# Eight weight matrices loaded as 32 runs of 16 KB and put in order by two block transpositions, in a kernel that streams 128 MB through one core

## The chip, the core and the metric

The kernel runs on one core of a Trainium2 chip. The metric is the device time of one execution in microseconds (us). Before the change it is 324.08 us, the median of 3 runs that lie between 323.89 and 324.3 us.

## What is computed

There are 128 images of 128 channels by 1024 columns in float32 (64 MiB in all), one subject number from 0 to 7 for each image, and eight weight matrices of 128x128 in float32, one for each subject. Each image is multiplied by the matrix of its subject, and the image itself is added:

```
w = weights[subjects]                        # B, C, D = 128, 128, 128
out = jnp.einsum('bct,bcd->bdt', x, w)       # T = 1024
x = x + out
```

The images are read once (67.1 MB) and the results are written once (67.1 MB). The eight matrices together are 0.5 MB.

## The kernel before, in words

The work goes in 32 turns of four images each (H = 2 halves of G = 2 images). A ring of 12 slots in SBUF (`x_all`, `xs`, 2 MB for each slot) holds the images: a turn's images are loaded into its slot, the result is written over them in place, and the slot is stored from there.

Two queues issue the DMAs. ScalarE (ACT) issues the loads, one for each image, through the helper `transfer` (L50), which passes the shapes of both sides to the DMA as they are written: on the side of DRAM an image is 32 rows of 16 KB, on the side of SBUF 128 partitions of 4 KB. The first 48 loads fill the 12 slots and wait for nothing; from turn 12 on ACT waits until a slot's store has landed (L200 to L203). SyncE (SP) issues, in this order: the 128 subject numbers (`given`, L179), the eight matrices (`w_all`, L180), and then the stores, each as soon as VectorE has added the half or the slot that it takes (L217). Most stores take a slot whole; the first and the last turn are stored in parts, and the last image by itself at the end (L238).

The matrices come with one `dma_start` into `w_all`: partition c holds row c of every matrix, which is 1024 pieces of 512 bytes. VectorE brings the subject numbers into range (L193 to L198), waits for the matrices (L222), reads the first four subject numbers into its registers (`subjects_of`) and copies the four matrices into the stationary tiles `ws` (`place`, L150 to L153). TensorE waits for the copy (`s_go`) and for the images (`s_ready`, which GpSimd passes on) and multiplies (`multiply`, L155); VectorE adds the product out of PSUM to the images in place (`add`, L170, L173), copies the matrices of the next turn (L152), and so on in a loop of 32 turns on each of the two engines (`nc.vector.Fori` at L226, `nc.tensor.Fori` at L231). Ahead of this TensorE multiplies zeros (L185) while nothing has landed yet.

The lines that the change and the steps of the prediction touch: the load of the matrices (L180), the wait for them (L222), the copies (L152), the operand of the multiplication (L161), and the issue of loads by ACT between L199 and L205.

Of the kernel before, what the change touches and what calls it, by code (L numbers as in the profile page):

```python
# [30 lines left out]
G = 2  # L31
H = 2
# [3 lines left out]
SLOTS = 12  # L36
# [3 lines left out]
DMA = 16  # L40
# [2 lines left out]

ROWS = 4

ALIGN = 4096
QUEUES = {mybir.EngineType.SP: "qSPDynamicHW", mybir.EngineType.Activation: "qActDynamicHW"}

# [21 lines left out]
@with_exitstack  # L70
def kernel(
    ctx: ExitStack,
    tc: tile.TileContext,
    x: bass.AP,
    subjects: bass.AP,
    weights: bass.AP,
    out: bass.AP,
):
    nc = tc.nc
    B, C, T = x.shape  # L80
    S, _, D = weights.shape
    NT = B // (G * H)

    def sbuf(name, *shape, dtype=F32):
        return ctx.enter_context(nc.sbuf_tensor(name, list(shape), dtype)).ap()


    room = -(nc.sbuf_base + -nc.sbuf_base % 32) % ALIGN
    if room:
        sbuf("room", C, room // 4)  # L90
    x_all = sbuf("x_all", C, SLOTS * H * G * T)
    xs = [
        x_all[:, i * H * G * T : (i + 1) * H * G * T].rearrange("c (q t) -> c q t", t=T)
        for i in range(SLOTS)
    ]
    w_all = sbuf("w_all", C, S, D)
    ws = [sbuf(f"w{i}", C, 1, D) for i in range(H * G)]
    zeros = sbuf("zeros", C, N)
    given, near, wrap = (sbuf(name, 1, B, dtype=I32) for name in ("given", "near", "wrap"))
    index = sbuf("index", 1, B + H * G, dtype=I32)  # L100
    ps = [
        ctx.enter_context(nc.psum_tensor(f"ps{i}", [D, G, T], F32)).ap() for i in range(P_SLOTS)
    ]

    s_given = tc.alloc_semaphore("s_given")
    s_wall = tc.alloc_semaphore("s_wall")
    s_index = tc.alloc_semaphore("s_index")
    s_zeros = tc.alloc_semaphore("s_zeros")
    s_product = tc.alloc_semaphore("s_product")
    s_added = tc.alloc_semaphore("s_added")  # L110

    s_ready = tc.alloc_semaphore("s_ready")
    s_go = tc.alloc_semaphore("s_go")

    s_slot = [tc.alloc_semaphore(f"s_slot{k}") for k in range(SLOTS)]
    s_head = tc.alloc_semaphore("s_head")
    s_first = tc.alloc_semaphore("s_first")

    def emptied(i):
        turns = i // SLOTS  # L120
        return DMA * (H * G + 1) * turns - (DMA * G if i >= SLOTS and i % SLOTS == 0 else 0)

    def load(engine, i, q):
        transfer(
            nc,
            engine,
            xs[i % SLOTS][:, q, :],
            x[i * H * G + q].rearrange("(a r) t -> a (r t)", r=ROWS),
        ).then_inc(s_head if i * H * G + q < G else s_slot[i % SLOTS], DMA)

    def store(i, q0, q1):
        b = i * H * G
        transfer(
            nc,
            nc.sync,
            out[b + q0 : b + q1].rearrange("g d t -> d g t"),
            xs[i % SLOTS][:, q0:q1, :].rearrange("d (o g) t -> d o (g t)", g=min(G, q1 - q0)),
        ).then_inc(s_first if i == 0 and q1 == G else s_slot[i % SLOTS], DMA)

    def subjects_of(i):  # L140
        _, subject = nc.values_load_multi_w_load_instructions(
            index[0:1, i] if isinstance(i, slice) else index[0:1, bass.ds(i * (H * G), H * G)],
            engines=[mybir.EngineType.DVE],
            min_val=0,
            max_val=S - 1,
            skip_runtime_bounds_check_because="the index is clamped on the chip above",
        )
        return subject

    def place(h, subject):  # L150
        for q in range(h * G, (h + 1) * G):
            copy = nc.vector.tensor_copy(ws[q], w_all[:, bass.ds(subject[q], 1), :])  # L152
        copy.then_inc(s_go, 1)  # L153

    def multiply(slot, h):  # L155
        nc.tensor.wait_ge(s_go, 1).then_inc(s_go, -1)
        nc.tensor.wait_ge(s_ready, 1).then_inc(s_ready, -1)  # L157
        for q in range(h * G, (h + 1) * G):
            for t in range(0, T, N):
                at = slot * (H * G * T) + (q * T + t)  # L160
                mm = nc.tensor.matmul(  # L161
                    ps[h][:, q % G, t : t + N],
                    ws[q][:, 0, :],
                    x_all[:, bass.ds(at, N)],
                    start=True,
                    stop=True,
                )
        mm.then_inc(s_product, 1)

    def add(slot, h):  # L170
        mine = x_all[:, bass.ds(slot * (H * G * T) + h * G * T, G * T)]
        nc.vector.wait_ge(s_product, 1).then_inc(s_product, -1)  # L172
        nc.vector.tensor_tensor(  # L173
            mine, ps[h].rearrange("d g t -> d (g t)"), mine, ALU.add
        ).then_inc(s_added, 1)

    with tc.tile_critical():  # L177

        nc.sync.dma_start(given, subjects.rearrange("(o b) -> o b", o=1)).then_inc(s_given, DMA)  # L179
        nc.sync.dma_start(w_all, weights.rearrange("s c d -> c s d")).then_inc(s_wall, DMA)  # L180

        nc.vector.memset(zeros, 0.0).then_inc(s_zeros, 1)  # L182
        nc.tensor.wait_ge(s_zeros, 1)
        for _ in range(IDLE):
            nc.tensor.matmul(  # L185
                ps[P_SLOTS - 1][:, G - 1, :N], zeros[:, :D], zeros, start=True, stop=True
            )

        nc.vector.memset(index[:, B:], 0).then_inc(s_index, 1)  # L192
        nc.vector.wait_ge(s_given, DMA)  # L193
        nc.vector.tensor_scalar(near, given, -S, S - 1, ALU.max, ALU.min).then_inc(s_index, 1)  # L194
        nc.vector.wait_ge(s_index, 2)
        nc.vector.tensor_scalar(wrap, near, 0, S, ALU.is_lt, ALU.mult).then_inc(s_index, 1)  # L196
        nc.vector.wait_ge(s_index, 3)
        nc.vector.tensor_tensor(index[:, :B], near, wrap, ALU.add).then_inc(s_index, 1)  # L198
        for i in range(NT):  # L199
            if i == SLOTS:  # L200
                nc.scalar.wait_ge(s_first, DMA)
            if i >= SLOTS:
                nc.scalar.wait_ge(s_slot[i % SLOTS], emptied(i))  # L203
            for q in range(H * G):
                load(nc.scalar, i, q)  # L205

        for i in range(NT):
            if i == 0:
                nc.gpsimd.wait_ge(s_head, DMA * G).then_inc(s_ready, 1)
                nc.gpsimd.wait_ge(s_slot[0], DMA * G).then_inc(s_ready, 1)  # L210
            else:
                nc.gpsimd.wait_ge(s_slot[i % SLOTS], emptied(i) + DMA * H * G).then_inc(s_ready, H)

        for i in range(NT):
            for h in range(H):
                if i in (0, NT - 1) or h == H - 1:
                    nc.sync.wait_ge(s_added, i * H + h + 1)  # L217
                    store(i, h * G if i in (0, NT - 1) else 0, (h + 1) * G - (i * H + h == NT * H - 1))


        nc.vector.wait_ge(s_index, 4)
        nc.vector.wait_ge(s_wall, DMA)  # L222
        subject = subjects_of(slice(0, H * G))
        for h in range(H):
            place(h, subject)
        with nc.vector.Fori(0, NT) as turn:  # L226
            subject = subjects_of(turn + 1)
            for h in range(H):
                add(turn % SLOTS, h)
                place(h, subject)  # L230
        with nc.tensor.Fori(0, NT) as turn:  # L231
            for h in range(H):
                multiply(turn % SLOTS, h)

    with tc.tile_critical() as waits:
        for i in range(NT - SLOTS, NT):
            nc.scalar.wait_ge(s_slot[i % SLOTS], emptied(i + SLOTS) + (DMA if i == NT - 1 else 0))
    last = nc.sync.dma_start(out[B - 1], xs[(NT - 1) % SLOTS][:, H * G - 1, :])  # L238

    tc.add_manual_dep(  # L240
        last.ins,
        waits.name,
        mybir.DependencyInfo(mybir.DependencyClass.NoSync, mybir.DependencyReason.SCHED_ONLY),
        reason="the end of the program waits for it",
    )
# [27 lines left out]
```

## Time and profile before

| | |
|---|---|
| median of 3 runs | 324.08 us |
| the profiled execution, its own time | 324.3 us |
| its span, from first to last instruction | 322.5 us |
| mean granted clock of TensorE | 0.92 |
| busy: TensorE, VectorE | 237.1 us (74%), 165.7 us (51%) |
| time that packets of the two DMA queues took, share of 16 engines' span | 50.0% (q1) and 49.5% (q10) |
| matrices: DMA issued, landed after | 1.35 us, 5.2 us |
| first and last copy of a matrix (L152) | 7.41 us, 281.1 us |
| first multiplication of an image (L161) | 8.56 us |
| first and last issue of a store | 16.40 us, 301.89 us |

The page of the profile is one execution on the chip. Its first part gives the busy time of each engine, the second cuts the span into 40 equal slices and writes the busy share of each in tenths (9 is 90% or more), with the share of the 16 DMA engines and the GB/s that they moved in two rows of their own. The third gives the DMA queues: packets, megabytes, and the time that their packets took as a share of the span of 16 engines. The DMA view can be asked for a stretch of time; it then cuts that stretch into 40 slices and counts the packets that started in it. The times in texts are microseconds from the start of the span.

The queue q1 is that of SP (subject numbers, matrices, stores), q10 that of ACT (images): q1 moved 67.64 MB, which is the 67.11 MB of the results and 0.53 MB of matrices and subject numbers; q10 moved the 67.12 MB of the images. A DMA is made of packets of data and, behind them, of packets of four bytes by which the engines that carried it report to its semaphore; the profile counts both.

### The profile page before, as it was taken

To read this page: it belongs to the slowest core of one execution; us is meant where nothing else is said; L and a number is where in the kernel's file an instruction comes from. 1 tells how busy PE (TensorE), PEld (TensorE's weight loads), DVE (VectorE), ACT (ScalarE), POOL (GpSimd) and SP (SyncE) were. 2 spreads that over 40 slices of the span, in tenths; PEclk is the share of its full clock that TensorE was granted. 3 is DMA by queue.
4 is the path that set the end of the run, shared out by engine and by line. 5 is a ranking of instruction groups with operands and counts; after the bars stand their busy time and mean duration, and the time that the engine had idled before them with its cause. 6 is when DMAs were issued, how large, how long until landed. Compare 5 with 4: busy or idle time off the path is not lost. (4 is left out here: it accounts for less than half of the span.)

```text
span 322.5 us, 2381 instructions
## 1 busy us (share of the span) xinstructions
PE 237.1 (74%) x518; PEld 98.1 (30%) x518; DVE 165.7 (51%) x202; POOL 0.2 (0%) x4
## 2 busy tenths in 40 slices
PE   5999998888888888888888888888885995500000
PEld 2434433333333333333333333333331432100000
DVE  2267776666566566666656655666666263600000
POOL 0000000000000000000000000000000000000000
PEclk9799999999999999999999999999999798955555
DMA  7999999999999999999999999999999999999996
GB/s 276 427 391 421 427 428 421 427 429 435 417 427 433 421 425 423 431 427 427 423 424 431 433 419 424 430 426 426 433 426 418 428 425 423 428 429 425 426 425 288
DMA packets 16067, 134.76 MB, mean 418 GB/s; under 512 B 2625, under 2 KB 3650, under 8 KB 3906
## 3 DMA queue, kind: packets, MB, share of 16 engines
q1 hardware_dynamic: 9922, 67.64, 50.0%
q10 hardware_dynamic: 6144, 67.12, 49.5%
q14 instruction: 1, 0.01, 0.0%
HBM read 67.63 MB, written 67.11 MB: 418 GB/s over the span
## 5 line engine op out<-in xcount | busy, mean ns | idle before, releaser
L161 PE MATMUL ps<-x_all,w 128*128 x512 | 232.7, 609 | 39.7 <-PEq L157 39.7
L173 DVE TENSOR_TENSOR x_all<-ps,x_all 128x2048 f32 x64 | 146.6, 2291 | 109.4 <-DVEq L172 109.4
L161 PEld LDWEIGHTS ps<-x_all,w 128*128 128x128 f32 x512 | 96.4, 193 | 176.0 <-issue 175.8
L152 DVE COPY w<-w_all 128x128 f32 x132 | 23.1, 218 | 4.2 <-DMA w_all<-in_L_cond_weights_dram 4.2
L185 PE MATMUL ps<-zeros 128*128 128x512 f32 x6 | 4.4, 890 | 1.7 <-DVE zeros L182 1.7
L185 PEld LDWEIGHTS ps<-zeros 128*128 128x128 f32 x6 | 1.7, 305 | 3.5 <-issue 1.9
L182 DVE MEMSET zeros<- 128x512 f32 x1 | 0.5, 485 | 1.0 <-SPq L177 1.0
L194 DVE TENSOR_SCALAR near<-given 1x128 int32<-1x128 int32 x1 | 0.2, 216 | 0.8 <-DMA given<-in_itok_B_dram 0.8
L198 DVE CUSTOM_DVE_ANT_0 index<-near,wrap 1x256 uint16<-1x256 uint16 x1 | 0.3, 278 | 0.0
L196 DVE TENSOR_SCALAR wrap<-near 1x128 int32<-1x128 int32 x1 | 0.2, 215 | 0.0
L260 POOL MEMSET const-bfloat16-1.0<- 128x1 bf16 x1 | 0.1, 101 | 0.0
L260 POOL MEMSET const-uint8-127<- 128x1 uint8 x1 | 0.1, 101 | 0.0
L260 POOL MEMSET const-float32-0.0<- 128x1 f32 x1 | 0.1, 98 | 0.2 <-issue 0.2
L260 POOL MEMSET const-float32-1.0<- 128x1 f32 x1 | 0.1, 98 | 0.0
L260 DVE BASE_LOAD x1 | 0.0, 15 | 0.1
L192 DVE MEMSET index<- 1x4 int32 x1 | 0.1, 62 | 0.0
## 6 DMA issues: line engine op xcount, KB each, us to landing
x_all<-in_x_dram ACTq DMA_DIRECT2D x128, 512.0 KB, 31.6
out_dram<-x_all SPq DMA_DIRECT2D x30, 2048.0 KB, 47.1
out_dram<-x_all SPq DMA_DIRECT2D x3, 1024.0 KB, 14.4
out_dram<-x_all SPq DMA_DIRECT2D x2, 512.0 KB, 20.6
w_all<-in_L_cond_weights_dram SPq DMA_DIRECT2D x1, 512.0 KB, 5.2
given<-in_itok_B_dram SPq DMA_DIRECT2D x1, 0.5 KB
```

The source lines that it names most:

```text
L152: copy = nc.vector.tensor_copy(ws[q], w_all[:, bass.ds(subject[q], 1), :])
L161: mm = nc.tensor.matmul(ps[h][:, q % G, t : t + N], ws[q][:, 0, :], x_all[:, bass.ds(at, N)], start=True, stop=True,)
L173: nc.vector.tensor_tensor(mine, ps[h].rearrange("d g t -> d (g t)"), mine, ALU.add).then_inc(s_added, 1)
L182: nc.vector.memset(zeros, 0.0).then_inc(s_zeros, 1)
L185: nc.tensor.matmul(ps[P_SLOTS - 1][:, G - 1, :N], zeros[:, :D], zeros, start=True, stop=True)
L192: nc.vector.memset(index[:, B:], 0).then_inc(s_index, 1)
L194: nc.vector.tensor_scalar(near, given, -S, S - 1, ALU.max, ALU.min).then_inc(s_index, 1)
L196: nc.vector.tensor_scalar(wrap, near, 0, S, ALU.is_lt, ALU.mult).then_inc(s_index, 1)
L198: nc.vector.tensor_tensor(index[:, :B], near, wrap, ALU.add).then_inc(s_index, 1)
L260: nc = _bacc.Bacc("TRN2", target_bir_lowering=False, num_devices=1)
```

## The change

The matrices are no longer loaded with row c of each in partition c. They are read in 32 runs of 16 KB (32 rows of a matrix, which lie side by side in DRAM, are one run; there are four such runs in each of eight matrices) through `transfer`, as the images are. On the side of DRAM the access is 4 by 8 runs of 16 KB, the four blocks of rows outermost and the eight matrices inside; on the side of SBUF it is 128 partitions of 4 KB, so that a run fills four partitions. Partition 32b + 4s + q then holds rows 32b + 8q to 32b + 8q + 7 of matrix s.

VectorE puts them in order. It transposes the 32x32 blocks of `w_runs` into `w_turned`, which lies in the last slot of the ring, waits for that, transposes the blocks back with their columns read in another order, and waits again. Row c of matrix s is then in partition c, in four pieces of 32 columns that lie 256 columns apart (`w_all`, the same memory as `w_runs`). `place` copies a matrix out of these four pieces. ACT waits for both transpositions before the loads of the last slot (turn 11), and the stationary tile is a plain 128x128.

```
+BLOCK = 32
...
-    w_all = sbuf("w_all", C, S, D)
-    ws = [sbuf(f"w{i}", C, 1, D) for i in range(H * G)]
+    w_runs = sbuf("w_runs", C, S * D)
+    w_all = w_runs.rearrange("c (h s l) -> c h s l", s=S, l=BLOCK)
+    w_turned = x_all[:, (SLOTS - 1) * H * G * T :][:, : S * D]
+    ws = [sbuf(f"w{i}", C, D) for i in range(H * G)]
...
-            copy = nc.vector.tensor_copy(ws[q], w_all[:, bass.ds(subject[q], 1), :])
+            copy = nc.vector.tensor_copy(
+                ws[q].rearrange("c (h o l) -> c h o l", o=1, l=BLOCK),
+                w_all[:, :, bass.ds(subject[q], 1), :],
+            )
...
-                    ws[q][:, 0, :],
+                    ws[q],
...
-        nc.sync.dma_start(w_all, weights.rearrange("s c d -> c s d")).then_inc(s_wall, DMA)
+        transfer(
+            nc,
+            nc.sync,
+            w_runs.rearrange("c (o f) -> c o f", o=1),
+            weights.rearrange("s (b r) d -> b s (r d)", r=BLOCK),
+        ).then_inc(s_wall, DMA)
...
+            if i == SLOTS - 1:
+                nc.scalar.wait_ge(s_wall, DMA + 2)
             if i == SLOTS:
                 nc.scalar.wait_ge(s_first, DMA)
...
         nc.vector.wait_ge(s_wall, DMA)
+        nc.vector.transpose(w_turned, w_runs).then_inc(s_wall, 1)
+        nc.vector.wait_ge(s_wall, DMA + 1)
+        nc.vector.transpose(
+            w_runs,
+            w_turned.rearrange("c (j a) -> c a j", j=RUN),
+        ).then_inc(s_wall, 1)
+        nc.vector.wait_ge(s_wall, DMA + 2)
         subject = subjects_of(slice(0, H * G))
```

## The prediction

> **What bounds the kernel now.** I first read the second and third parts of the page, because the kernel moves 134.76 MB and computes little.
>
> ```profile
> PE   5999998888888888888888888888885995500000
> ...
> DMA  7999999999999999999999999999999999999996
> ...
> DMA packets 16067, 134.76 MB, mean 418 GB/s; under 512 B 2625, under 2 KB 3650, under 8 KB 3906
> ...
> q1 hardware_dynamic: 9922, 67.64, 50.0%
> q10 hardware_dynamic: 6144, 67.12, 49.5%
> ```
>
> The 16 DMA engines are full in every slice but the first and the last, and the two queues' packets take 50.0 + 49.5 = 99.5% of 16 engines' whole span. TensorE has nothing left to do in the last five slices. So the end is not set by a chain of instructions (the chain of waits reaches back only to 278.56 us and shows nothing but small steps): it is set by how long the busiest DMA engine needs for the packets given to it. The table of stages says the same: from 281 to 322.5 us VectorE is busy for 0.30 us and TensorE not at all, while DMA runs at 399 GB/s. The stores are some 40 us behind the computation, and that is cover for anything that is late at the start.
>
> Next I asked the DMA view for three stretches: the matrices alone, a stretch of loads alone, and the end.
>
> ```profile
> DMA packets 1083, 0.97 MB, mean 358 GB/s; under 512 B 32, under 2 KB 1056, under 8 KB 1056
> ...
> q1 hardware_dynamic: 1040, 0.52, 65.1%
> ```
>
> This is 3.6 to 6.3 us. All 1040 packets of the matrices (1024 of 512 bytes, 16 that report) are in it and took 65.1% of 16 x 2.7 us = 28.1 us, or **1.76 us on each of 16 engines**.
>
> ```profile
> DMA packets 383, 4.19 MB, mean 419 GB/s; under 512 B 127, under 2 KB 127, under 8 KB 127
> ...
> q10 hardware_dynamic: 383, 4.19, 98.7%
> ```
>
> This is 6.3 to 16.3 us, loads of images alone: 383 - 127 = 256 packets of 16 KB in 98.7% of 160 us, 157.9 us, so **0.617 us for one 16 KB packet** (reports counted in).
>
> ```profile
> DMA  7399796998997999989989989977433212011000
> ...
> q1 hardware_dynamic: 321, 1.20, 73.0%
> ```
>
> This is 317 to 321 us in slices of 0.1 us. At 319.7 us the share falls to four tenths, and at 320.8 us it reaches nothing: most engines finish by about 319.8 us, and a few go on for about 1 us. The engines end that close to each other, after 320 us of work each, because every large DMA gives each engine the same share.
>
> **The load of the matrices.** It loses 1024 packets of 512 bytes and gains 32 of 16 KB. Whether this gains or loses depends on how many engines carry the 32 runs, which no row shows directly; the packet counts bound it. There are 2625 packets under 512 bytes. The issues listed on the page are 128 loads, 35 stores and the matrices, 164 DMAs, and 164 x 16 = 2624. The one packet that is left is the report of `given`. So 164 DMAs ran on 16 engines, and one ran on a single engine. What sets them apart is the outermost count of their accesses: the loads have 32 on one side and 128 on the other, the stores and the old matrices 128, `given` has 1. The new load has 128 in SBUF but **4 in DRAM** (the blocks of rows outermost). Its ends are then 4 engines with 8 runs each, if the outermost count is what is dealt out, and 16 engines with 2 runs each, if all 32 runs are, as in an image's load.
>
> - 4 engines: 8 x 0.617 = 4.94 us on each, where 1.76 us was: +3.18 us on four engines, -1.76 us on the twelve others.
> - 16 engines: 2 x 0.617 = 1.23 us on each: -0.53 us on all.
>
> I take 4: in every row the number of engines goes with the outermost counts, and a count of 4 on one side is nearer to the 1 of `given` than to the 32 of an image's load.
>
> The Trainium skill (DMA: Bandwidth & Descriptors, "Why a DMA increments its semaphore by 16 and not by 1") says that each side's slowest dimension that isn't 1 is looked at, and that the largest number up to 16 that divides both is the number of engines. By that rule the new load gets 4, and the trace agrees with it for 128 with 32 (16 engines) and for `given` (one). The same page ("Specifications") gives 512 bytes as enough for full rate; by it the old pieces would have cost 1.23 us like large ones, and the sum would be +3.71 us with 4 engines and nothing with 16. The trace does not agree, as 1.76 us is 43% more than 1.23 us, and the trace decides.
>
> **What the other engines can take over.** Nothing: which engine carries which part of an image is settled by the image's shape, so the four that are behind stay behind through all 128 loads and 35 stores, and both queues have work waiting throughout (a load lands 31.6 us after its issue, a store 47.1 us, by the medians on the page). The end moves by +3.18 us if the engine that ends last is one of the four, and by 3.18 less the 1.1 us of spread, about +2.1 us, if they are among the early ones. I take the middle, **+2.6 us**.
>
> **The two transpositions.** No row shows one. Each handles 1024 elements in a partition. By the fill of zeros (512 elements in 485 ns) it would take 0.97 us, by the addition (2048 in 2291 ns) 1.15 us, by the copy of a matrix (128 in 218 ns) 1.74 us: two of them 1.9 to 3.5 us. I take 2.3 us, by the addition, which is the row of nearest length. They lie between the landing of the matrices and the first copy. If the matrices go through back to back, as they do now, they land 8.7 to 9 us from the start instead of 6.55 (1.35 + 5.2); if they take turns with packets of images, by about 14 us. The first copy now comes 0.86 us after the landing, and the first multiplication 1.15 us after that copy. The first multiplication moves from 8.56 us to 13.3 us (9.0 + 2.3 + 0.86 + 1.15), or to 18 us at worst, and the first store from 16.40 us to 21 or 26 us. **Cost: nothing.** It is hidden by the loads, of which 48 are free to go: 25.2 MB, 60 us at 419 GB/s. By 26 us less than half of that has landed. Without this cover it would cost those 5 to 10 us. Late first stores let the loads run further ahead, and the same bytes follow at the end.
>
> **The waits.** VectorE's two new waits hold up only its own copies, which the last paragraph prices. ACT's wait before turn 11 stands ahead of loads 45 to 128. ACT issues 14 loads in 9.10 us, 0.65 us each, and reaches this wait at 0.9 + 44 x 0.65 = 29.5 us; the transpositions are over by 12 to 17 us. Cost nothing; if they came after 29.5 us there would still be a queue of loads issued and not carried out. SP's stores stand behind no new wait.
>
> **The copies.** 132 copies of 218 ns read four pieces of 32 columns instead of one of 128. No row shows such a copy. Below, nothing changes; above, I allow a doubling, 4 x 0.22 = 0.9 us more in a turn. A turn is about 10 us (320 over 32), of which VectorE works 165.7 / 32 = 5.2 us. Hidden by DMA, cost nothing; if DMA weren't the bound it would cost up to 28 us in all, as TensorE waits for the copies. The plain stationary tile changes no count.
>
> **The sum.** 324.3 us of the profiled execution + 2.6 = 326.9 us; the median lies 0.2 us lower, so **326.7 us**.
>
> **The rivals.**
>
> 1. All 16 engines carry the runs, two each, as they carry an image's 32. For it: the same helper, the same size of run, and 32 runs can be dealt out to 16. Against it: the outermost count, and `given`. It gives 324.08 - 0.53 = 323.5 us, not slower. The point at which the change turns from gain to loss is 1.76 / 0.617 = 2.9 runs on the busiest engine: up to two runs gain, three or more lose. With eight engines (four runs, 2.47 us) it would be +0.7 us, 324.8 us.
> 2. The limit is one that the engines share, not one of each: then four engines left alone at the end would go faster, and the 4.9 us by which they trail the twelve (3.18 + 1.76) would shrink. For it: loads alone (419 GB/s) and loads with stores (427 GB/s, 60 to 268 us) run at nearly one rate. Against it: 512 KB in small packets ran well below that rate (1.76 us an engine is 298 GB/s) and nothing filled the gap. With the last 4.9 us at double speed the end would come 2.4 us earlier, at 324.3 us.
> 3. The runs of the four engines run into other engines' writes to the same partitions, as each run fills four partitions that an image's share also fills. No row shows two engines on one partition. A run would take up to twice 0.617 us: +4.94 us more, 331.6 us.
> 4. The late start gets through to the end: product and first store 5 to 10 us late. It decides only where it exceeds the 40 us by which the stores trail; it would give up to 334 us. Everything in the stages after 281 us speaks against it.
>
> **How the numbers follow.** Four engines, end moved by 2.0 to 3.6 us: 0.72, the forecast, with a range of its own of 326.0 to 327.7 us. Sixteen engines: 0.13. Eight engines or a shared limit, 324.1 to 325.5 us: 0.07. Collisions or a start that gets through, 328 to 334 us: 0.08. The range is 323.4 to 328.5 us: it needs the other side as well to hold 8 in 10 safely, since the bounds of the number of engines are its ends. A measurement of this kernel can tell about 0.2%, 0.65 us, from no change. Faster by more than that needs 323.43 us or less, which only the lower edge of rival 1 reaches: 0.04. Within it: the rest of rival 1 and half of the eight engines: 0.13. Slower: 0.83.
>
> **What would show it.** With four engines q1 has 9922 - 1040 + 32 + 4 = 8918 packets and 2613 are under 512 bytes; with sixteen, 8930 and 2625. With four the stretch before the end has about 5 us in which the DMA share is near a quarter, and the matrices land about 7.5 us or more after their issue. Two transpositions of 1 to 1.7 us stand ahead of a first multiplication at 13 to 18 us, and TensorE and VectorE still have nothing to do in the last 35 us. The forecast is wrong if the matrices run on 16 engines, or if four lagging engines catch up before the end.

## The result, and the profile after

The changed kernel takes 332.84 us (median of 5 runs, 332.29 to 333.1) against 323.89 us before (5 runs, 323.77 to 324.3): 1.0274 times as long, 95% interval 1.0264 to 1.0285, or 8.95 us more. The forecast was 326.7 us, slower, with a range up to 328.5 us: the sign was right, and the size was a third of what came. The profiled execution took 332.87 us with a span of 331.1 us, 8.6 us more than the span before.

The page of the kernel before has this row, in slices of 8.06 us:

```profile
GB/s 276 427 391 421 427 428 421 427 429 435 417 427 433 421 425 423 431 427 427 423 424 431 433 419 424 430 426 426 433 426 418 428 425 423 428 429 425 426 425 288
```

The page of the changed kernel, first the rows of the slices and of the DMA queues, then the groups that are new:

```profile
DMA  6999999999999999999999999999999999999993
GB/s 180 238 374 424 420 434 421 426 427 425 428 428 425 428 427 424 426 428 427 426 428 424 424 437 417 427 437 423 424 422 437 416 421 428 427 427 427 427 423 161
DMA packets 15063, 134.76 MB, mean 407 GB/s; under 512 B 2613, under 2 KB 2614, under 8 KB 2870
...
q1 hardware_dynamic: 8918, 67.64, 48.8%
...
L161 DVE COPY w<-w_runs 128x128 f32 x132 | 23.2, 219 | 0.8 <-DVE w_runs L247 0.8
L245 DVE STREAM_TRANSPOSE x_all<-w_runs 128x1024 f32<-128x1024 f32 x1 | 1.2, 1245 | 16.6 <-DMA w_runs<-in_L_cond_weights_dram 16.6
...
L247 DVE STREAM_TRANSPOSE w_runs<-x_all 128x1024 f32<-128x1024 f32 x1 | 1.9, 1915 | 0.0
```

The number of engines is in the packet counts: 8918 on q1 and 2613 under 512 bytes are the numbers worked out for four engines; sixteen would have left 8930 and 2625. What no step of mine had is in the GB/s: DMA is full from the second slice on, as before, but the first three slices (8.3 us each) move 180, 238 and 374 GB/s, where it was 276, 427 and 391. In the second of them the engines are busy all the time and move little more than half as much. VectorE waits 16.6 us for the matrices (first transposition at 19.57 us), the first multiplication comes at 24.44 us and the first store at 33.78 us.

The DMA view from 4 to 18 us, before and after:

```profile
DMA packets 1469, 5.90 MB, mean 422 GB/s; under 512 B 173, under 2 KB 1139, under 8 KB 1139
...
q10 hardware_dynamic: 487, 5.41, 91.4%
```

```profile
DMA packets 266, 3.16 MB, mean 226 GB/s; under 512 B 73, under 2 KB 73, under 8 KB 73
## 3 DMA queue, kind: packets, MB, share of 16 engines
q10 hardware_dynamic: 235, 2.70, 83.4%
q1 hardware_dynamic: 31, 0.46, 13.7%
```

After the change the images' queue has 2.70 MB, 165 packets of 16 KB, in 83.4% of 16 x 14 us = 186.8 us: **1.13 us for a packet** that took 0.617 us before. The matrices' queue has 28 of its 32 runs in 13.7%, 30.7 us: 1.10 us for a run. In these 14 us 5.90 - 3.16 = 2.74 MB less were moved, which at 422 GB/s is 6.5 us of all 16 engines. From 18 us on the rate is 419 GB/s again.

The end of the changed kernel, 320 to 331.1 us in slices of 0.28 us:

```profile
DMA  9997999999999999853332212122222221000000
```

The share falls below a half at about 324.9 us, as twelve engines finish (at 319.8 us before, by the row in the prediction), and stays near two tenths, which is some four engines in sixteen, until about 329.3 us. So four engines do trail, by some 4.4 us, where 4.94 us was worked out. But the twelve end 5.1 us later than before, where they were to end 1.76 us earlier.

### The profile page after: what moved, and what is told of

It is laid out like the page before. It is cut to its first block, busy times and chain, and to the rows that moved or that the text cites. A ratio compares the mean times of both kernels' runs of the same rounds, so it can differ in the third digit from the quotient of the medians.

```text
span 331.1 us, 2383 instructions
## 1 busy us (share of the span) xinstructions
PE 241.9 (73%) x518; PEld 100.0 (30%) x518; DVE 168.9 (51%) x204; POOL 0.2 (0%) x4
## 2 busy tenths in 40 slices
DMA packets 15063, 134.76 MB, mean 407 GB/s; under 512 B 2613, under 2 KB 2614, under 8 KB 2870
## 3 DMA queue, kind: packets, MB, share of 16 engines
q1 hardware_dynamic: 8918, 67.64, 48.8%
## 5 line engine op out<-in xcount | busy, mean ns | idle before, releaser
L173 PE MATMUL ps<-x_all,w 128*128 x512 | 236.6, 619 | 43.7 <-PEq L169 26.2
L173 PEld LDWEIGHTS ps<-x_all,w 128*128 128x128 f32 x512 | 98.2, 197 | 182.7 <-issue 182.3
L161 DVE COPY w<-w_runs 128x128 f32 x132 | 23.2, 219 | 0.8 <-DVE w_runs L247 0.8
L245 DVE STREAM_TRANSPOSE x_all<-w_runs 128x1024 f32<-128x1024 f32 x1 | 1.2, 1245 | 16.6 <-DMA w_runs<-in_L_cond_weights_dram 16.6
L202 PE MATMUL ps<-zeros 128*128 128x512 f32 x6 | 5.3, 1057 | 1.7 <-DVE zeros L199 1.7
L247 DVE STREAM_TRANSPOSE w_runs<-x_all 128x1024 f32<-128x1024 f32 x1 | 1.9, 1915 | 0.0
```

The source lines that it names most:

```text
L161: copy = nc.vector.tensor_copy(ws[q].rearrange("c (h o l) -> c h o l", o=1, l=BLOCK), w_all[:, :, bass.ds(subject[q], 1), :],)
L173: mm = nc.tensor.matmul(ps[h][:, q % G, t : t + N], ws[q], x_all[:, bass.ds(at, N)], start=True, stop=True,)
L202: nc.tensor.matmul(ps[P_SLOTS - 1][:, G - 1, :N], zeros[:, :D], zeros, start=True, stop=True)
L245: nc.vector.transpose(w_turned, w_runs).then_inc(s_wall, 1)
L247: nc.vector.transpose(w_runs, w_turned.rearrange("c (j a) -> c a j", j=RUN),).then_inc(s_wall, 1)
```

## Experiments

The theory to test first, A: the whole loss lies in the load on four engines, and nothing else of the change costs anything. Its rivals put some of it on the transpositions and copies or on the late start.

**All of the change but its load.** The old load is kept, and the second transposition reads the columns as they then lie.

```
-        transfer(... w_runs, weights.rearrange("s (b r) d -> b s (r d)", r=BLOCK))
+        nc.sync.dma_start(
+            w_runs.rearrange("c (s d) -> c s d", s=S), weights.rearrange("s c d -> c s d"))
...
-            w_turned.rearrange("c (j a) -> c a j", j=RUN),
+            w_turned.rearrange("c (s h l) -> c h s l", s=S, l=BLOCK),
```

> All of the change but its load: the matrices come as before, 1024 pieces of 512 bytes on 16 engines, and the two transpositions, their waits, ACT's wait and the copies out of four pieces stay (the second transposition reads the columns in the order that this needs). Theory A (the whole loss lies in the load on four engines): within 0.2% of before, 323.3 to 324.5 us, though the first multiplication comes about 4 us later. Rival B (part of the loss lies in the later start or in the copies): 325 us or more.

323.73 us against 323.81 us for the kernel before on the same chip, ratio 1.0004 (0.9995 to 1.0014; the ratios come from all runs and are not quotients of the two medians). The first multiplication comes at 10.74 us. The transpositions, the four-piece copies (218 ns) and the waits cost nothing that can be measured.

**The late start alone.**

```
+            if i == SLOTS - 1:
+                nc.scalar.wait_ge(s_wall, DMA + 4)
...
         nc.vector.wait_ge(s_wall, DMA)
+        for k in range(4):
+            nc.vector.memset(x_all[:, (SLOTS - 1) * H * G * T :], 0.0).then_inc(s_wall, 1)
+            nc.vector.wait_ge(s_wall, DMA + k + 1)
```

> Before, with four fills of the last slot (about 3.9 us each) on VectorE ahead of the first copy of a matrix, so that the first multiplication comes at about 24 us, as after the change, and not at 8.6 us; nothing else is changed. Theory A (the stores trail by 40 us, so a late start costs nothing): 323.3 to 325 us. Rival B (the late first store leaves DMA work for later that isn't made up): up to 16 us more, 332 us or above would put the whole loss here.

Its timeline from 20 to 35 us (start, length, engine, line):

```profile
25.61 9.57 PE L161 MATMUL ps<-x_all,w 128*128 x16 [18.64 <-DVE w L152]
...
34.38 0.65 SPq L57 DMA_DIRECT2D out_dram<-x_all  x1
```

The first multiplication and the first store are as late as after the change, or later, and the time is 323.9 us against 323.81, ratio 1.0006 (0.9996 to 1.0015). The late start is shown to cost nothing: the loads that are free to go cover it, as the prediction had it. The rivals of theory A fall.

**The same matrices on sixteen engines**, in the right order (blocks of 8 rows outermost, 4 KB pieces, with the copies and the second transposition fitted to them), and the same 32 runs on sixteen engines, in the order in which they lie in DRAM (this kernel leaves out the order that the products need).

```
-            weights.rearrange("s (b r) d -> b s (r d)", r=BLOCK),
+            weights.rearrange("s (a r) d -> a s (r d)", r=RUN),        # first kernel
...
+            weights.rearrange("s (b r) d -> (s b) (r d)", r=BLOCK),    # second kernel
```

> The changed kernel with its load cut so that the outermost count is 16: 16 blocks of 8 rows by 8 matrices, 128 pieces of 4 KB, which fill one partition each; the transpositions and their order of columns are fitted to that, the result is the reference's. Theory A (outermost count 4 gave four engines, 16 gives sixteen): q1 has 9922 - 1040 + 128 + 16 = 9026 packets, each engine has 8 x 0.159 us (a 4 KB packet by the last store) = 1.27 us instead of 1.76 us, and the time is 0.5 us under before: 323.2 to 323.6 us. Rival B (the order of rows or the transpositions cost): 325 us or more.

> The changed kernel with the same 32 runs of 16 KB, but the access in DRAM written as 32 by 16 KB with the matrices outermost, as an image's load is written; rows of the matrices then end up in other partitions, so the products are of other matrices than the reference's. Theory A (the number of engines follows the outermost count): 16 engines, two runs each, 8930 packets on q1, packets of 0.62 us, 323.2 to 323.8 us. Rival B (it is the size of the runs, or their four partitions, that slows the packets): packets of about 1 us for the images beside them, and 327 us or more.

The page of the second kernel:

```profile
DMA packets 15075, 134.76 MB, mean 419 GB/s; under 512 B 2625, under 2 KB 2626, under 8 KB 2882
...
q1 hardware_dynamic: 8930, 67.64, 50.0%
```

Both ran on sixteen engines (9026 packets on q1 for the first, 8930 for the second). The loss is gone: 323.99 us, ratio 1.0006 (0.9997 to 1.0015), and 323.42 us, ratio 0.9994 (0.9984 to 1.0003), each against 323.81 us. Long contiguous runs cost nothing as such; the loss comes with the outermost count of 4. The hoped-for gain of 0.5 us is not there in the first and not clear of zero in the second. The packets of the first took 0.156 to 0.41 us by their own records, 0.231 us in the mean, and 8 x 0.231 = 1.85 us an engine is no less than the old 1.76 us.

That leaves why packets slowed down. Theory P: an engine that writes to partitions which another engine is filling slows both. Rival R: the reads in DRAM get in each other's way. The next five kernels are the one before with the change's load issued **in addition**, to different places; its data is not used, and ACT waits for it ahead of the slots that it lands in.

```
+        transfer(nc, nc.sync, PLACE,
+            weights.rearrange("s (b r) d -> b s (r d)", r=32)).then_inc(s_more, DMA)
...
+            if i == SLOTS - 1:                        # - 2 for the partition ranges
+                nc.scalar.wait_ge(s_more, DMA)
```

PLACE is 128 partitions of 4 KB as in the change; partitions 0 to 15, 64 to 79 or 32 to 47 with 32 KB each; or a scratch tensor in DRAM.

> Before, with the change's load issued in addition, behind the matrices on SP, into the last slot (4 by 8 runs of 16 KB on four engines, 128 partitions of 4 KB), and ACT waiting for it before the loads of that slot. Its data is not used. The change lost 8.95 us although it removed 1.76 us an engine, so by every theory this costs about 8.95 + 1.76 = 10.7 us: 334 to 335 us, with packets of 0.8 to 1.6 us beside it, where an image's take 0.62 us. It is the base for the next three.

> As the last, but the 32 runs go to partitions 0 to 15 (two runs to each), so that each of the four engines writes four partitions of its own the whole time and no two of the four go to the same group of partitions. Theory P (packets slow each other where several engines write to the same group of partitions at a time): fewer engines meet, so packets nearer to 0.62 us; if none meet, 8 x 0.62 = 4.9 us more than before, 328 to 329 us. Rival R (the reads in DRAM slow each other): unchanged, 334 to 335 us.

> As the last, but partitions 64 to 79. Theory P: each of the four engines again keeps to four partitions of its own; if these are partitions that other engines fill with images, and those of the last run are the four engines' own, this one is slower than the last run, 330 to 335 us. Rival R (reads in DRAM): 334 to 335 us, as more4. If both partition ranges give 328 to 329 us, only meetings among the four matter.

> As more4, with the same reads on the same four engines, but written to a scratch tensor in DRAM instead of SBUF. Theory P: no meeting in SBUF, packets of images keep 0.62 us, and the end moves by 8 packets on four engines, about 5 us if a packet to DRAM takes as long: 328 to 330 us. Rival R (reads in DRAM): packets of images at 1 us and more, 333 us or above.

> As more4_low and more4_high, but partitions 32 to 47. Theory P in its sharper form (an image's load gives each engine groups of four partitions, and those 32 apart to the same engine, so partitions 0 to 15 and 32 to 47 are the four engines' own and 64 to 79 are not): 328.2 us, as more4_low, with packets of 0.611 us. If partitions 32 to 47 belong to other engines: 332.7 us, as more4_high.

| where the 32 runs go | us | against before | ratio, 95% interval |
|---|---|---|---|
| 128 partitions, as in the change | 334.08 | 323.81 | 1.0314 (1.0296 to 1.0331) |
| partitions 64 to 79 | 332.71 | 323.81 | 1.0277 (1.026 to 1.0294) |
| partitions 0 to 15 | 328.23 | 323.81 | 1.014 (1.0123 to 1.0157) |
| partitions 32 to 47 | 328.27 | 323.71 | 1.0142 (1.0123 to 1.016) |
| DRAM | 328.17 | 323.81 | 1.0135 (1.0118 to 1.0152) |

The DMA view of each from 6.4 to 15 us (queue, packets, MB, share of 16 engines), first with 128 partitions, then partitions 64 to 79, then 0 to 15, then DRAM:

```profile
q10 hardware_dynamic: 179, 1.93, 89.7%
q1 hardware_dynamic: 20, 0.33, 15.0%
```

```profile
q10 hardware_dynamic: 195, 2.10, 89.4%
q1 hardware_dynamic: 22, 0.36, 14.8%
```

```profile
q10 hardware_dynamic: 288, 3.15, 86.0%
q1 hardware_dynamic: 32, 0.52, 14.2%
```

```profile
q10 hardware_dynamic: 288, 3.15, 86.0%
q1 hardware_dynamic: 33, 0.52, 14.2%
```

The share hardly differs, the megabytes do. An image packet took 1.05 us (89.7% of 137.6 us over 1.93 MB in packets of 16 KB), 0.96 us, 0.62 us and 0.62 us; a run took 1.03, 0.93, 0.61 and 0.61 us. With the same reads, the writes to DRAM slow nothing, so rival R falls. The partition ranges differ in nothing but which partitions they are: 0 to 15 and 32 to 47 are as harmless as DRAM (the view of partitions 32 to 47 has the same two lines as that of 0 to 15), 64 to 79 cost twice as much. Theory P stands, in its sharper form: partitions 0 to 15 and 32 to 47 behave as the four engines' own, 64 to 79 as others'. The Trainium skill (DMA: Bandwidth & Descriptors, "The descriptor swizzle") deals groups of four partitions to engines in this way, those 32 apart to the same engine and those from 64 up to eight other engines. The trace names no engine, but the three ranges agree with it.

Where nothing meets, the additional load costs 4.4 us (328.23 - 323.81): 8 runs x 0.617 = 4.94 us, less some of the spread at the end. Without the 1.76 us of the old load, which stays in these kernels, an estimate is 2.7 us, and the prediction had 2.6 us: its sum holds where nothing meets.

**Eight engines; the runs without images; and sixteen engines with each run on the engine's own partitions.**

```
-            weights.rearrange("s (b r) d -> b s (r d)", r=BLOCK),
+            weights.rearrange("s (b r) d -> (s b) (r d)", r=BLOCK).rearrange("(e k) f -> e k f", e=8),
```

```
+            if i == 0:
+                nc.scalar.wait_ge(s_wall, DMA)      # the change; images held back
```

```
+            w_runs.rearrange("c (o f) -> c o f", o=RUN // ROWS),
+            weights.rearrange("s (a r) d -> a s (r d)", r=ROWS),     # 32 blocks of 4 rows, 2 KB pieces
...
```

> The changed kernel with its 32 runs dealt out to eight engines (outermost count 8 in DRAM, four runs each, in the order in which they lie in DRAM, so rows of the matrices end up in other partitions and the products are of other matrices than the reference's). Without meetings the sum would be 4 x 0.617 - 1.76 = 0.7 us: 324.3 to 324.7 us. Theory P: each engine again fills 16 partitions in turn, most of them other engines', so packets of 0.8 us and more and a loss that is well over 0.7 us, 326 to 331 us.

> The changed kernel with ACT's first load held until the matrices have landed, so that the 32 runs have the engines to themselves. Theory P1 (runs of the four engines also meet each other, as blocks 0 and 1 fill partitions 32 apart at the same step, which one image engine fills): packets of about 1.2 us, landing about 10 us after the first packet. Theory P2 (they meet only images): 0.61 us, landing 5 us after the first packet. The images then start late by that time, so the kernel's time is 330 us by P2 and 335 us by P1.

> The changed kernel with blocks of 4 rows outermost (32 of them) by 8 matrices, 256 pieces of 2 KB, so that 16 engines carry them and each fills the same partitions as with an image; the second transposition goes in two halves to fit this order, the result is the reference's. Theory P: no meetings, packets at a steady length of about 0.08 to 0.09 us, 16 x 0.085 = 1.4 us an engine instead of 1.76 us: 0.3 to 0.4 us under before, 323.3 to 323.6 us, hardly beyond what can be measured. If packets vary as in the 4 KB version (0.16 to 0.4 us there), the partitions are not matched as I think.

Eight engines: 327.82 us against 323.71, ratio 1.0132 (1.0115 to 1.0148), and 0.94 us for a run by the packets' records. It is 4.1 us where 0.7 was worked out without meetings: P again.

The runs without images, 2.8 to 10.4 us:

```profile
DMA  9003000720029002252006302224204022020000
...
q1 hardware_dynamic: 36, 0.52, 21.5%
```

21.5% of 121.6 us over 32 runs is 0.82 us for a run, between the two expectations: by their records the first three took 1.43 to 1.45 us and most of the late ones 0.616 us. That fits four engines that meet each other too while they are in step, and less once they aren't; which packets met, the records don't say. With 333.58 us against 323.71 (1.0306, 1.0285 to 1.0327) the kernel pays for the images' late start instead; holding the images back is no remedy.

Sixteen engines with 2 KB pieces, and so with the partitions dealt as for an image: 324.07 us against 323.71, ratio 1.0011 (1.0002 to 1.002). Nearly all of its pieces took 0.084 us, the mean is 0.090 us, 1.44 us an engine, as worked out and steadier than the 4 KB pieces, and still nothing is gained. No version beats the kernel before beyond what can be measured.

**Does a meeting slow engines that have no part in it?** 32 pairs of packets at double length are 32 x 2 x 0.617 = 39 us of engine time, 2.5 us for each of 16; the loss in the changed kernel was 6.5 us for each. Two last kernels put one and two engines on others' partitions: 12 runs to partitions 64 to 67 with outermost counts of 3 and 4, and 32 runs to partitions 64 to 71 with counts of 2 and 8.

```
+        transfer(nc, nc.sync,
+            x_all[64:68, (SLOTS - 3) * H * G * T :].rearrange("c (o f) -> c o f", o=3),
+            weights.rearrange("s (b r) d -> (s b) (r d)", r=32)[:12].rearrange("(e k) f -> e k f", e=3))
```

> Before, with 12 runs of 16 KB in addition, whose outermost counts (3 in DRAM, 4 in SBUF) have no common divisor, so that one engine should carry them all (its reports: one packet under 512 bytes), into partitions 64 to 67. Local theory L (a meeting slows only the two engines that write to the same partitions): two of 16 engines have long packets, so some 12% of the image packets beside the runs lie above 0.7 us. Spreading theory S (it also slows engines that write elsewhere): far more than 12%. The engine ends 12 runs later, 7 us if a run takes 0.61 us and 15 us if it takes 1.23 us: 330 to 338 us by both.

> The same with 32 runs on two engines (outermost counts 2 and 8), 16 each, into partitions 64 to 71, four of them for each engine. Local theory L: four of 16 engines are slowed, some 25% of the image packets lie above 0.7 us. Spreading theory S: well over 25%, as with more4_high, where three quarters were slow although eight engines at most shared partitions. The two engines end 16 runs later: 333 to 343 us by both.

The page of each, and its DMA view from 6.4 to 15 us, first with one engine:

```profile
DMA packets 16080, 134.96 MB, mean 405 GB/s; under 512 B 2626, under 2 KB 3651, under 8 KB 3907
```

```profile
q10 hardware_dynamic: 312, 3.41, 96.1%
```

```profile
DMA packets 16101, 135.29 MB, mean 400 GB/s; under 512 B 2627, under 2 KB 3652, under 8 KB 3908
```

```profile
q10 hardware_dynamic: 220, 2.39, 96.4%
```

One and two packets more under 512 bytes than the 2625 of before: one engine and two engines. With one, an image packet takes 0.64 us (96.1% of 137.6 us over 3.41 MB). By the records of this stretch, 182 image packets were in flight beside a run, and 12 of them took more than 0.7 us, one in fifteen: as many as one other engine carries, which is the local theory. With two, an image packet takes 0.91 us, and 113 of 146 took more than 0.7 us (77%): far more than four engines in sixteen. In the kernel with partitions 64 to 79 it was 120 of 128. In the kernel before it is none, up to 18 us. Later packets can't be counted in this way: between 18 and 22 us, with no runs at all, 34 of 81 image packets of the kernel before are above 0.7 us, from a cause that no run here looks for.

The ends say the same. The DMA view from 317 to 333 us in slices of 0.4 us, first with one engine:

```profile
DMA  7999998321001001010100000000000000000000
```

```profile
DMA  9989989989999998999996322011011010101101
```

With one, the share falls at 319.8 us, as in the kernel before; then by the records two packets are in flight until about 325.2 us and one until 331.7 us. So fourteen engines lost nothing, one ended some 5 us late, and one, with the 12 runs, some 11 us late. With two, all sixteen are full until 325.4 us, where the kernel before had fallen off at 319.8 us, and two packets are in flight until 336.7 us. So a single meeting stays with its two engines, while two at a time, and four, reach engines that write elsewhere. That is shown; by what path it spreads is not, and stays open. The times, 334.67 us (1.0336, 1.0306 to 1.0366) and 339.81 us (1.0495, 1.0465 to 1.0526) against 323.77, lie within what was expected of engines that end 12 and 16 runs later.

## Why the prediction was wrong, step by step

- **What bounds the kernel**: right. The busiest DMA engines set the end; the late start and VectorE's work cost nothing, each shown alone.
- **Four engines and not sixteen**: right, by the packet counts, and the rule held for outermost counts of 4, 8, 16, 32, 2 with 8, and 3 with 4 (one engine). "16 engines: -0.53 us" was not found: at most 0.5 us of gain lies in the interval of the second sixteen-engine kernel.
- **"+3.18 us on four engines, -1.76 us on the twelve others"**: the step that failed. The difference between the two, 4.94 us, was nearly right (some 4.4 us in the trace). But the step took 0.617 us as the price of a 16 KB packet whatever it meets, and put at nothing what the engines do to each other. For 14 us a run took 1.10 us and an image packet 1.13 us (151 of 165 took more than 0.7 us, so nearly all engines were slowed), and the mean engine lost 6.5 us. Put together: 6.5 us of all, plus 3.3 us by which the four end after the mean engine (12/16 of the 4.4 us lag), less up to 1.1 us of spread is 8.7 us or somewhat more, near the 8.6 us of the spans.
- **Rival 3** named this mechanism, with 331.6 us, and shared 0.08 with another. It lengthened the four engines' runs alone; that nearly all image packets beside them are lengthened too is what it lacked. "No row shows two engines on one partition" was true of the profile before. But the change makes one engine fill 32 partitions in a row, where an image's load deals each engine a sixteenth of the partitions; that could be read from the shapes, and it made the rival likelier than I put it.
- **Rival 2**, a limit that the engines share, fell: alone at the end, the four didn't make up their lag. **Rival 4**, the late start, fell by experiment.
- **The transpositions**: 1.25 and 1.92 us, 3.16 us together, where 2.3 us was taken between 1.9 and 3.5. **The start**: first multiplication at 24.44 us, past the 18 us given as the worst, because the runs landed that much later. Neither reached the end. **Copies and waits**: 219 ns and no cost, right.

## What to carry to other kernels

Before a transfer is given longer runs, read the outermost count of both sides: it deals the work to the DMA engines, and where all engines are full, the one with the most decides. Then compare which partitions each engine fills with what the other loads of that time give it: a 0.5 MB load on four engines cost 10.3 us on top of everything where it crossed them and 4.4 us on its engines' own partitions, and in place of the old load, dealt like the others, it made no difference. A duration taken from a row holds for the traffic that the row was in.

## What the runs showed of the hardware

- Four engines that write to other engines' partitions lengthen nearly all 16 KB packets in flight, from 0.61 to about 1.05 us in the mean (0.96 us with partitions 64 to 79); one engine that does so slows about one image packet in fifteen.
- A block transposition of 128x1024 in float32 takes 1245 ns, also where it reads pieces of 32 contiguous columns in another order; reading single columns 512 bytes apart it takes 1915 ns, and 2007 ns in the order of the 4 KB version.
- Pieces of 512 bytes, 2 KB, 4 KB and 16 KB of the matrices took 0.027, 0.084, 0.159 and 0.611 us most often. Two thirds of the 4 KB pieces, whose partitions aren't dealt as an image's, took longer, up to 0.41 us.
